# Layer 0's front reordered, and batch 1's second norm in smaller steps, in a two-layer transformer kernel on one core

## The chip, the core and the metric

The kernel runs on one core of a Trainium2 chip. The core has five engines that run side by side, each with its own in-order instruction queue: PE (TensorE, matrix products), DVE (VectorE, arithmetic on rows), ACT (ScalarE, functions and scaled copies), POOL (GpSimd, arithmetic on rows) and SP (SyncE, which here issues DMAs). PE writes to PSUM, a small memory of which the kernel uses eight banks; everything else lies in SBUF. DMA engines move data between the device's memory and SBUF, and also transpose tiles within SBUF. Loads and transposes are issued on SP's queue, weight loads on POOL's, and the stores of the result on ACT's.

The metric is the device time of the whole launch in microseconds (us), as the median of several runs; a profile is one execution more, with a record of every instruction.

## What is computed

Two batches of 1024 rows of 512 numbers pass through two layers. Each layer normalises its rows and adds an attention and a second branch to the input:

```python
xn = _layernorm(x)
x = x + _L0_attn_ref(xn, ...) + _L0_ffn_ref(xn, ...)
xn = _layernorm(x)
x = x + _L1_attn_ref(xn, ...) + _L1_ffn_ref(xn, ...)
```

Layer 0's attention has one head of width 128. Its second branch scales rows by their root mean square, forms 24 logits per row, runs 50 Sinkhorn steps on 16 of them (a 4 x 4 mixing matrix per row) and softmaxes on the others, and mixes four streams of 128 columns:

```python
x_norm = x * jax.lax.rsqrt(jnp.mean(x * x, axis=-1, keepdims=True) + RMS_EPS)
H_res = sinkhorn_log((x_norm @ W_res.T).reshape(B, T, n, n) + H_res_base)
y = jnp.einsum('btnc,btn->btc', x_streams, H_pre) @ W_branch
x_mixed = jnp.einsum('btij,btjc->btic', H_res, x_streams)
return (x_mixed + jnp.einsum('btc,btn->btnc', y, H_post)).reshape(B, T, nC)
```

Layer 1's attention has 32 query heads in 8 groups. Its queries attend over blocks of rows, causally; keys and values come from a compressed latent (`Wk_down`, `Wv_down`, then `Wk_up`, `Wv_up`). Its second branch is a dense product and a LoRA of 8 experts with two chosen per row by a small router (`gw1`, a norm, `gw2`, top 2); the router counts the rows of each expert over both batches and drops an expert's weights where a count is above the capacity:

```python
h = jax.nn.relu(layernorm(xf @ gw1.T + gb1) * ln_gamma + ln_beta)
top_v, top_i = jax.lax.top_k(h @ gw2.T + gb2, K)
counts = onehot.sum(axis=0)
allowed = (counts <= capacity).astype(xf.dtype)
main = xf @ weight.T
lora = jnp.einsum('enr,ero->no', tmp, lora_B) * ALPHA
```

## The kernel before

**Numbers.** Matrix operands are pairs of 16-bit halves, a high and a low part. A product is three passes (`mm3`, L89): high x high, high x low, low x high. So every operand costs a high part (a copy to 16 bits) and a low part (the difference). Weights are split on POOL by `split_pool` (L95 to L97: scale, high, low); results are split out of PSUM by `evac` (L105 on ACT, L106 on DVE).

**Tiles.** Each batch has eight tiles of 128 rows, kept in SBUF as `acc[b, t]`. A layer norm takes statistics of a tile (L220, L221), then parameters for several tiles at once (`layernorm_tiles`, L222 to L225, with `rsqrt`, L202 to L207: logarithm and exponential on ACT and one Newton step of four DVE operations). `normed_T` (L234 to L243) makes the normalised tile on ACT, POOL or DVE, its high part on ACT (L239), its low part on POOL or DVE (L241), and issues the transpose (L243) on SP's queue.

**Layer 0.** `front0` loads, normalises and transposes a batch (batch 0 in two halves of four tiles, `F0`), computes the 24 logits and the values V (L403, L106), then Q and K. `split_w0a` and `split_w0b` split the layer's weights; `lat_weights` loads (L674) and splits Wlat, which layer 1's latents use. `branch0` is the second branch's product with `W_branch` (PE, ACT L455, POOL L456 and L460), `branch0_add` adds it to the tiles on POOL (L469, L473). `attn0_rows` and `attn0_out` are the attention in two halves of 512 rows: scores, minimum of the negated scores (L288), exponential (L292), high part (L319 to L322), low part (L328 on POOL, L330 on DVE), transposes (L335), product with V, product with Wo, sum into `acc` (L506). The Sinkhorn iterations of batch 0 (`chain_dve`, L594 to L601) run on DVE, a step at a time between other work, with the matrix kept in a PSUM bank; those of batch 1 run on POOL during layer 1. After the chain, `mix0_units` mixes the streams of batch 0 (ACT L651, POOL L652, DVE L660), and the second norm of batch 0 follows in two halves (`LG`).

**Layer 1.** `layer1_attn` walks 16 groups (8 of each batch) of 32 steps; a step is `row_step`, 32 rows of four heads. Behind each step stands a list of other work at fixed places: projections, splits, the products with V and Wo, and everything in `extra`, entered by `put(h, s, f)` at step `s` counted from the start. So steps 192 to 223 are group 6, and 224 to 255 group 7, the last of batch 0. In this way batch 1's Sinkhorn chain and mixing, its second norm (`late_norm`, at step `LN1`), its router (tiles at `G1`, transposed tiles by `tile_of`, products `gating_h` three steps on by `GL`, ten steps of `gating`), the router's sum over both batches (`weights_of`, step `WT`), the transposed tiles that the attention needs (`xT_tile`, from `LX`), Wlat's splits (`lat_w`) and latents (`lat_unit`, from `LA`), and the dense branch's weights (`ffn_fetch`, `ffn_split`, `FW`) and blocks (`ffn_block`, `FF`) are all spread behind rows of batch 0.

**Order.** The program is written in this order, but a planner sorts the instructions of each engine before the launch; it may pull a ready instruction forward. Two tools bind it. `after(i)` lets what is written inside it be issued only behind `i`. `behind(i, j, True)` makes instruction `i` wait for `j`. `last_low` is the last low part made by DVE (L330). In `parts_of`, `mix0_units` and `ffn_split`, POOL's first operation already stands behind it.

**Buffers.** Tiles come from rings named by a tag: `f2k` has four buffers (weight staging, normalised tiles), `wo` nine, `xr` and `wq` four, `PT` three. In PSUM `pp` has three banks, `s` four, and `av` one, used by `out_tile`. A ring is handed out in the written order, so a new tile waits until the one that had its buffer before is read.

Of the kernel before, what the change touches and what calls it, by code (L numbers as in the profile page):

```python
# [16 lines left out]
P = 128  # L17
S = 1024
NB = 2
NT = S // P  # L20
# [19 lines left out]
SK0, SKN, MX0, MXN, LN1 = 1, 116, 122, 74, 198  # L40

G0, G1, GL, WT, LX, LA = 16, 200, 3, 220, 231, 240
# [3 lines left out]
FW, FF = 210, 221  # L46
# [6 lines left out]
def tile_model(ctx: ExitStack, tc: tile.TileContext, out: bass.AP, a: dict):  # L53
# [116 lines left out]
    def split_w0b():  # L170
        evac(st_qk, wqk0[:, :, 0, :], wqk0[:, :, 1, :], 8.0)
        A.activation(bqkv, bqkv, AF.Copy, scale=32.0)
        split_pool(st_o[:, 0:P], wb0[:, 0], wb0[:, 1], 32.0)
        split_pool(st_o[:, P:], wo0[:, 0], wo0[:, 1], 32.0)
        split_pool(bo_st, bo[:, 0], bo[:, 1], 32.0)
# [23 lines left out]
    def rsqrt(y, ve, tag):  # L199

        t = T(tag, list(ve.shape), bufs=2)
        A.activation(t, ve, AF.Ln)  # L202
        A.activation(y, t, AF.Exp, scale=-0.5)
        V.tensor_tensor(t, y, y, ALU.mult)
        V.tensor_tensor(t, t, ve, ALU.mult)
        V.tensor_scalar(t, t, -0.5, 1.5, ALU.mult, ALU.add)
        V.tensor_tensor(y, y, t, ALU.mult)  # L207
# [7 lines left out]
    def layernorm_tiles(b, mv, rs, ts):  # L215
        ve = T("ve", [P, NT], bufs=2)
        sl = slice(ts[0], ts[-1] + 1)
        for t in ts:
            st = T("bnst", [P, 6], bufs=2)
            V.bn_stats(st, acc[b, t])  # L220
            V.bn_aggr(mv[:, t, :], st)  # L221
        V.tensor_scalar(ve[:, sl], mv[:, sl, 1], LN_EPS, None, ALU.add)  # L222
        rsqrt(rs[:, 0, sl], ve[:, sl], "rs")
# [4 lines left out]
    def normed_T(b, mv, rs, t, dst, pool, tags=(("f2k", FB), ("wo", WB))):  # L228
# [6 lines left out]
        elif pool:  # L235
            G.tensor_scalar(xf, acc[b, t], rs[:, 2, t:t + 1], rs[:, 1, t:t + 1], ALU.mult, ALU.add)
# [4 lines left out]
        lo = eng.tensor_tensor(hl[:, :, 1, :], xn, hl[:, :, 0, :], ALU.subtract)  # L241
        (last_pool if eng is G else last_lo)[0] = lo
        last_T[0] = nc.sync.dma_start_transpose(dst, hl.rearrange("p c l d -> p (c l d)"))  # L243
# [126 lines left out]

    def front0(b, between=lambda: None):
        mv, rs = layernorm(b, "a")
        xT = T("xT", [P, NT, 2 * NC, P], F16, bufs=1)
        for ts in F0[b]:
            layernorm_tiles(b, mv, rs, ts)
# [13 lines left out]

        ms = T("rms", [P, NT], bufs=2)  # L390
        V.tensor_tensor(ms, rs[:, 0], rs[:, 0], ALU.mult)
        V.tensor_tensor(ms, ms, mv[:, :, 1], ALU.mult)
        V.tensor_scalar(ms, ms, RMS_EPS, None, ALU.add)
        rf = T("rf", [P, NT], bufs=2)
        rsqrt(rf, ms, "rs")
        V.tensor_scalar(rf, rf, 1.0 / 1024.0, None, ALU.mult)
        lg = T("lg", [P, NT, 24], bufs=1)
        Vh = T("V", [P, NT, 2, P], F16, bufs=2)
        for t in range(NT):
# [3 lines left out]
            V.scalar_tensor_tensor(lg[:, t, :], p[:, 128:152], rf[:, t:t + 1], base24,  # L403
                                   ALU.mult, ALU.add)
# [264 lines left out]
    def lat_weights():  # L669

        wl = T("PT", [P, 4, 2, NC, P], F16, bufs=3)
        for mc in range(4):
            st = T("f2k", [P, NC, P], bufs=FB)
            nc.gpsimd.dma_start(st, a["Wlat"][mc])  # L674
            split_pool(st, wl[:, mc, 0], wl[:, mc, 1], 32.0)
# [17 lines left out]
    def lat_w(mc):  # L693
        st = T("f2k", [P, NC, P], bufs=FB)
        nc.gpsimd.dma_start(st, a["Wlat"][mc])
        w1 = T("wo", [P, 2, NC, P], F16, bufs=WB)
        split_pool(st, w1[:, 0], w1[:, 1], 32.0)
        return w1
# [330 lines left out]
    def xT_tile(b, t, pool):  # L1029
        normed_T(b, *ln1[b], t, xT1[b][:, t], pool, (("f2k", FB), ("wo", WB)) if b else  # L1030
                 (("xr", XB), ("wo", WB)))

    def tile_of(b, t):
        d = T("wo", [P, 2 * NC, P], F16, bufs=WB)
        normed_T(b, *ln1[b], t, d, True, (("f2k", FB), ("xr", XB)))
# [28 lines left out]

    def late_norm():
        ln1[1] = layernorm(1, "b")
        layernorm_tiles(1, *ln1[1], range(NT))
# [14 lines left out]
    for t in range(NT):  # L1082
        for k, f in enumerate(mix0_units(1, t, f0[1][5], True)):
            put(0, MX0 + MXN * (4 * t + max(k - 1, 0)) // 32, f)
    for t in range(NT):
# [10 lines left out]
    for b, s in ((0, G0), (1, G1)):  # L1096
        put(0, s, lambda b=b: gate_start(b))
        for t in range(NT):
            if b == 0:
                put(0, s + t, lambda t=t: gating_h(hs[0], t, gw1, xT1[0][:, t]))  # L1100
            else:
                put(0, s + t, lambda t=t: dts.update({t: tile_of(1, t)}))
# [73 lines left out]
```

## Time and profile before

| | us |
|---|---|
| median of three runs (1847.12 to 1853.01) | 1851.1 |
| the profiled execution | 1847.95 |
| its span, first to last instruction | 1846.2 |
| PE busy | 1708.2 |
| DVE busy | 1473.1 |
| ACT busy | 1191.1 |
| POOL busy | 896.5 |

The mean granted clock of TensorE is 0.976 of full speed. Layer 0 takes about the first 223 us, and layer 1's rows the rest. Some marks on the way, each the start of an instruction group in the trace:

| | us |
|---|---|
| first statistics (L220) | 3.34 |
| first normalised tile (L238) | 15.04 |
| first transpose issued (L243) | 20.22 |
| first product of Q and K | 35.19 |
| first Sinkhorn operation of batch 0 (L527) | 38.50 |
| last Sinkhorn operation of batch 0 (L610) | 194.14 |
| PE starts layer 1's latents | 223.43 |
| parameters of batch 1's second norm ready (POOL starts L236) | 846.98 |
| first product of the dense branch | 921.88 |

A line of the page or the trace gives a start or a share, an engine, a line of the kernel, the operation, what it writes and reads with shapes, and in brackets how long the engine had been idle before and what ended that. In lines of stretches the columns are the stretch, its length, busy time and count of PE, PE's weight loads, DVE, ACT and POOL, then the granted clock, the DMA engines' share and GB/s. Where an operation line has a count above one, its duration is from the first start to the last end.

### The profile page before, as it was taken

Reading aid. Unit: us, or ns where it says so; the run is one execution under the profiler, and the core shown is the slowest. Engines: PE = TensorE matmul, PEld = TensorE weight load, DVE = VectorE, ACT = ScalarE, POOL = GpSimd, SP = SyncE. Lnnn points to the kernel's source line nnn. Section 1 sums busy time; section 2 is a strip of 40 time slices with the busy share of each in tenths; the row PEclk is TensorE's granted clock in tenths of the full one; section 3 lists DMA queues with packets and bytes.
Section 4 is the critical chain, followed back from the end, with each engine's and each line's share of the span. In section 5 each row is a group of like instructions: output and inputs, shape, how many; then the busy total and the mean of one; then the engine's idle time right before and its main releaser. Section 6 shows DMA issues by size and latency. Waiting matters only on the chain.

```text
span 1846.2 us, 35059 instructions
## 1 busy us (share of the span) xinstructions
PE 1708.2 (93%) x11394; PEld 1038.5 (56%) x11394; DVE 1473.1 (80%) x4162; ACT 1191.1 (65%) x2917; POOL 896.5 (49%) x1476
## 2 busy tenths in 40 slices
PE   4666389999999999998999999999999999999998
PEld 2434146566666566655555566666666666666565
DVE  8888968988888878778976768778787877787675
ACT  4848666656676778876544656667666767676564
POOL 5568629778766465647634433323242424235200
PEclk9888699999999999999999999999999999999999
DMA  7435225656575656468645656556566655566455
GB/s 212 82 56 132 59 44 123 151 118 139 119 149 98 141 128 144 105 142 143 146 98 125 144 126 140 135 124 141 125 134 124 142 118 142 124 143 135 97 121 118
DMA packets 693482, 230.25 MB, mean 125 GB/s; under 512 B 674081, under 2 KB 674209, under 8 KB 693298
## 3 DMA queue, kind: packets, MB, share of 16 engines
q1 hardware_dynamic: 677842, 180.75, 47.3%
q0 software_dynamic: 13152, 43.07, 8.7%
q10 hardware_dynamic: 2304, 4.20, 0.7%
q8 instruction: 89, 1.46, 0.3%
q14 instruction: 95, 0.78, 0.1%
HBM read 52.81 MB, written 4.19 MB: 31 GB/s over the span
## 4 chain that ended last, share of the span: by engine, by line
PE 47%; DVE 2%; DMA 1%; POOL 1%; issue 1%; ACT 0%; SPq 0%; DVEq 0%
PE pp L89 26%; PE av L365 11%; PE s L89 10%; DVE Phl L330 0%; DVE f2k L913 0%; DMA f2k<-in_Wq 0%; DMA xT<-wo 0%; DVE P L288 0%; POOL wo L241 0%; DMA PT<-Phl 0%; POOL f2k L95 0%; SPq L335 0%; DVE P L284 0%; DMA twT<-twhl 0%; DVE Q L106 0%
## 5 line engine op out<-in xcount | busy, mean ns | idle before, releaser
L292 ACT ACTIVATE P<-P,nm 128x1024 f32<-128x1024 f32 (+31 forms) x528 | 391.5, 742 | 280.9 <-DVE nm L284 263.4
L330 DVE SCALAR_TENSOR_TENSOR Phl<-P,r,Phl 128x64 f16<-128x64 f32 (+16 forms) x627 | 460.8, 759 | 75.7 <-ACT Phl L322 70.3
L89 PE MATMUL s<-K,Q 128*128 128x512 f16 (+22 forms) x2400 | 439.1, 317 | 19.7 <-DVE P L288 11.7
L365 PE MATMUL av<-PT,V 128*128 128x256 f16 x3456 | 425.6, 274 | 9.4 <-DMA PT<-Phl 8.5
L365 PEld LDWEIGHTS <-V 128*128 128x128 f16 x3456 | 338.2, 98 | 92.9 <-DMA PT<-Phl 10.6
L322 ACT ACTIVATE Phl<-P,r 128x1024 f16<-128x1024 f32 (+31 forms) x515 | 369.5, 730 | 20.6 <-DMA PT<-Phl 5.3
L89 PE MATMUL pp<-xT,wq 128*128 128x512 f16 x1536 | 371.8, 381 | 4.5 <-DVE Q L106 2.3
L89 PE MATMUL pp<-wo,ao 128*128 128x512 f16 x1536 | 369.9, 379 | 2.0 <-ACT ao L105 1.9
L95 POOL TENSOR_SCALAR f2k<-f2k 128x512 f32<-128x512 f32 x164 | 113.9, 695 | 500.6 <-DVE Phl L330 458.9
L89 PEld LDWEIGHTS <-Q 128*128 128x128 f16 x2400 | 222.8, 98 | 175.7 <-issue 27.7
L89 PEld LDWEIGHTS <-wq 128*128 128x128 f16 x1536 | 149.7, 98 | 172.6 <-issue 6.8
L89 PEld LDWEIGHTS <-ao 128*128 128x128 f16 x1536 | 149.5, 98 | 156.9 <-ACT ao L105 3.4
L284 DVE CUSTOM_DVE_ANT_0 P<-s,mask,nm 128x272 f32<-128x272 f32 (+15 forms) x256 | 157.3, 615 | 9.3 <-PE s L89 1.0
L288 DVE TENSOR_SCALAR_CACHE_REDUCE P<-s 128x512 f32<-128x512 f32 (+15 forms) x272 | 152.6, 562 | 13.4 <-PE s L89 11.2
L316 DVE RECIPROCAL r<-r 128x1 f32<-128x1 f32 x528 | 78.9, 154 | 87.5 <-ACT P L292 84.5
L317 ACT ACTIVATE r<-r 128x1 f32<-128x1 f32 x528 | 95.6, 192 | 60.2 <-DVE r L316 59.7
L105 ACT ACTIVATE ao<-av 128x512 f16<-128x512 f32 x128 | 74.9, 585 | 81.7 <-PE av L365 81.5
L334 POOL MEMSET Phl<- 128x192 f16 (+1 forms) x320 | 56.2, 189 | 142.3 <-DMA PT<-Phl 97.3
L105 ACT ACTIVATE Q<-pp 128x512 f16<-128x512 f32 x128 | 74.6, 583 | 64.3 <-PE pp L89 60.0
L284 DVE CUSTOM_DVE_ANT_0 P<-s,mask 128x32 f32<-128x32 f32 (+15 forms) x256 | 103.7, 430 | 14.9 <-PE s L89 14.2
L755 DVE SCALAR_TENSOR_TENSOR acc<-pp,acc 128x512 f32<-128x512 f32 x128 | 87.1, 681 | 35.1 <-PE pp L89 34.7
L106 DVE SCALAR_TENSOR_TENSOR Q<-pp,Q 128x512 f16<-128x512 f32 x128 | 87.4, 683 | 34.0 <-ACT Q L105 33.7
(256 smaller groups left out, 2153.1 us busy)
## 6 DMA issues: line engine op xcount, KB each, us to landing
f2k<-in_Wq POOLq DMA_DIRECT2D x64, 256.0 KB, 3.1
f2k<-in_WoT POOLq DMA_DIRECT2D x64, 256.0 KB, 3.3
PT<-Phl SPq DMA_TRANSPOSE x528, 3.2
acc<-in_x SPq DMA_DIRECT2D x16, 256.0 KB, 5.1
f2k<-in_Wup POOLq DMA_DIRECT2D x16, 256.0 KB, 3.3
out<-acc ACTq DMA_DIRECT2D x16, 256.0 KB, 3.5
xr<-V SPq DMA_DIRECT2D x32, 128.0 KB, 2.4
xr<-in_x SPq DMA_DIRECT2D x12, 256.0 KB, 3.9
```

Of the source, the lines that this page charges most:

```text
L89: nc.tensor.matmul(dst, lhs(l), rhs(r), start=(i == 0 and j == 0), stop=(i == n - 1 and j == 2))
L95: first = G.tensor_scalar(stage, stage, scale, 1.0, ALU.mult, ALU.mult)
L105: A.activation(hl_hi, src, AF.Copy, scale=scale)
L106: return V.scalar_tensor_tensor(hl_lo, src, scale, hl_hi, ALU.mult, ALU.subtract)
L284: last_row[0] = V.tensor_tensor_reduce(Pm[:, o:o + w], pt[:, :w], mask[:, 512 - w:], -scale, first, ALU.add, ALU.min, nm[:, k:k + 1])
L288: last_row[0] = V.tensor_scalar(Pm[:, o:o + w], pt[:, :w], -scale, first, ALU.mult, ALU.min, accum_out=nm[:, k:k + 1])
L292: A.activation(Pm[:, :W], Pm[:, :W], AF.Exp, bias=last, scale=-1.0, accum_out=r[:, 0:1])
L317: A.activation(r[:, 1:2], r[:, 1:2], AF.Copy, scale=PSCALE)
L322: A.activation(hl[1], Pm[:, :W], AF.Copy, scale=r[:, 1:2])
L330: last_low[0] = V.scalar_tensor_tensor(lo, Pm[:, a0:a1], r[:, 1:2], hi[:, a0:a1], ALU.mult, ALU.subtract)
L365: nc.tensor.matmul(p, v, pt, start=(k == 0), stop=(k == len(todo) - 1))
L755: V.scalar_tensor_tensor(acc[b, t], p, 1.0 / 256.0, acc[b, t], ALU.mult, ALU.add)
```

## The change

In layer 0's front:

- The loads of Wlat wait for the parameters of the first four tiles (`first_norm`), and the first operation of each of its splits waits for the last logits of batch 0 (`last_lg`). The splits of W_branch, Wo and bo wait for the same logits.
- The statistics of tiles 4 to 7 of batch 0 may be issued only behind the parameters of tiles 0 to 3.
- The root mean square's factor `rf` is computed right behind the last parameters, before the tiles that use them are normalised.
- `rsqrt` has a second form: the exponential goes to a tile in PSUM (tag `av`) and three `scalar_tensor_tensor` operations follow in place of four. `layernorm_tiles` uses it except for batch 1's second norm, and `rf` uses it.

In batch 1's second norm:

- The statistics of a tile are entered three steps after the last mixing step of the tile (`late_stats`); the parameters move from step 198 to 197.
- The router's tiles start at the steps of `G1` (198 to 207, one step left free at 202 and 206) and not at 200 to 207. Tiles 1, 4 and 7 are normalised on ACT (`GP`), the others on POOL, where they now stand behind `last_low`.
- `normed_T` has a second step, `later`: the low part and its transpose are entered one step further on; a low part on POOL stands behind `last_low`. This holds for the router's tiles and for `xT_tile` of batch 1.
- The ten steps of the router start at 210 and not at 211; `weights_of` moves from 220 to 221, the dense blocks from 221 to 222, the dense weights of batch 0 from 210 to 220 by twos to 210, 212, 213, 215, 216, 218, each fetched two steps earlier.
- Wlat's loads are entered two steps ahead of its splits, and the splits are made by `parts_of`, whose first operation stands behind `last_low`.

```diff
-SK0, SKN, MX0, MXN, LN1 = 1, 116, 122, 74, 198
-G0, G1, GL, WT, LX, LA = 16, 200, 3, 220, 231, 240
+SK0, SKN, MX0, MXN, LN1 = 1, 116, 122, 74, 197
+G0, GL, WT, LX, LA = 16, 2, 221, 231, 240
+G1 = (198, 199, 200, 201, 203, 204, 205, 207)
+GP = (1, 2, 1, 1, 2, 1, 1, 2)
+G2 = 210
-FW, FF = 210, 221
+FW, FF = ((210, 212, 213, 215, 216, 218), tuple(8 * 58 + 2 + 2 * k for k in range(6))), 222
...
-        split_pool(st_o[:, 0:P], wb0[:, 0], wb0[:, 1], 32.0)
-        split_pool(st_o[:, P:], wo0[:, 0], wo0[:, 1], 32.0)
-        split_pool(bo_st, bo[:, 0], bo[:, 1], 32.0)
+        for args in ((st_o[:, 0:P], wb0[:, 0], wb0[:, 1]), (st_o[:, P:], wo0[:, 0], wo0[:, 1]),
+                     (bo_st, bo[:, 0], bo[:, 1])):
+            behind(split_pool(*args, 32.0), last_lg[0], True)
...
-    def rsqrt(y, ve, tag):
+    def rsqrt(y, ve, tag, ps=False):
...
+        if ps:
+            r = out_tile()[:, :ve.shape[1]]
+            A.activation(t, ve, AF.Ln)
+            A.activation(r, t, AF.Exp, scale=-0.5)
+            V.scalar_tensor_tensor(t, r, -0.5, ve, ALU.mult, ALU.mult)
+            V.scalar_tensor_tensor(t, r, 1.0, t, ALU.mult, ALU.mult)
+            V.scalar_tensor_tensor(y, t, 1.5, r, ALU.add, ALU.mult)
+            return
...
+    def layernorm_tile(b, mv, t):
+        st = T("bnst", [P, 6], bufs=2)
+        V.bn_stats(st, acc[b, t])
+        V.bn_aggr(mv[:, t, :], st)
+
+    def layernorm_tiles(b, mv, rs, ts, late=False):
...
+        for t in () if late else ts:
+            layernorm_tile(b, mv, t)
         V.tensor_scalar(ve[:, sl], mv[:, sl, 1], LN_EPS, None, ALU.add)
-        rsqrt(rs[:, 0, sl], ve[:, sl], "rs")
+        rsqrt(rs[:, 0, sl], ve[:, sl], "rs", not late)
...
-            G.tensor_scalar(xf, acc[b, t], rs[:, 2, t:t + 1], rs[:, 1, t:t + 1], ALU.mult, ALU.add)
+            xg = G.tensor_scalar(xf, acc[b, t], rs[:, 2, t:t + 1], rs[:, 1, t:t + 1], ALU.mult, ALU.add)
+            if later is not None:
+                behind(xg, last_low[0], True)
...
+        def low():
+            lo = eng.tensor_tensor(hl[:, :, 1, :], xn, hl[:, :, 0, :], ALU.subtract)
+            if eng is G and later is not None:
+                behind(lo, last_low[0], True)
+            (last_pool if eng is G else last_lo)[0] = lo
+            last_T[0] = nc.sync.dma_start_transpose(dst, hl.rearrange("p c l d -> p (c l d)"))
+
+        if later is None:
+            low()
+        else:
+            later(low)
...
         for ts in F0[b]:
-            layernorm_tiles(b, mv, rs, ts)
+            with after(*stt):
+                stt = [layernorm_tiles(b, mv, rs, ts)]
+            first_norm.append(stt[0])
+            if ts[-1] == NT - 1:
...
+                rsqrt(rf, ms, "rs", True)
...
-            nc.gpsimd.dma_start(st, a["Wlat"][mc])
-            split_pool(st, wl[:, mc, 0], wl[:, mc, 1], 32.0)
+            load = nc.gpsimd.dma_start(st, a["Wlat"][mc])
+            first = split_pool(st, wl[:, mc, 0], wl[:, mc, 1], 32.0)
+            behind(load, first_norm[0], True)
+            behind(first, last_lg[0], True)
...
+        put(0, MX0 + MXN * (4 * t + 3) // 32 + 3, lambda t=t: late_stats(t))
...
-                put(0, s + t, lambda t=t: dts.update({t: tile_of(1, t)}))
-                put(0, s + t + GL, lambda t=t: gating_h(hs[1], t, gw1, dts[t]))
+                put(0, G1[t], lambda t=t: dts.update({t: tile_of(1, t, lambda f: lows.update({t: f}))}))
+                put(0, G1[t] + 1, lambda t=t: lows.pop(t)())
+                put(0, G1[t] + GL + 1, lambda t=t: gating_h(hs[1], t, gw1, dts[t]))
...
-        put(0, LX + t, lambda t=t: xT_tile(1, t, t % 2 == 1))
+        put(0, LX + t, lambda t=t: xT_tile(1, t, t % 2 == 1, lambda f: lows.update({t: f})))
+        put(0, LX + t + 1, lambda t=t: lows.pop(t)())
...
-        put(0, LA + 2 * mc - 4, lambda mc=mc: lw.update({mc: lat_w(mc)}))
+        put(0, LA + 2 * mc - 6, lambda mc=mc: lw.update({mc: fetch(a["Wlat"][mc])}))
+        put(0, LA + 2 * mc - 4, lambda mc=mc: lw.update({mc: lat_w(lw[mc])}))
```

## The prediction

> **What bounds the kernel now.** I read the page's 40 slices first, then the busy time by stretches, then what PE (TensorE) waits for, then the instructions of single stretches in order of time.
>
> ```profile
> PE   4666389999999999998999999999999999999998
> DVE  8888968988888878778976768778787877787675
> sum 360.00, PE 248.88 PEld 145.19 DVE 308.33 ACT 220.27 POOL 231.27; mean PE 10.82 PEld 6.31 DVE 13.41 ACT 9.58 POOL 10.06
> 200.00:220.00 20.00, 0.00 (x0) 0.00 (x0) 19.16 (x60) 17.29 (x55) 14.13 (x12) 0.50 0.19 37
> ...
> sum 290.00, PE 275.12 PEld 162.92 DVE 224.76 ACT 172.33 POOL 147.29; mean PE 9.49 PEld 5.62 DVE 7.75 ACT 5.94 POOL 5.08
> ```
>
> PE is busy 1708.2 of 1846.2 us, so 138 us idle can be had at all. The first sum covers 0 to 360 us: PE idle 360 - 248.9 = 111 us there, with DVE (VectorE) at 308 of 360 and at 19.16 of 20 where PE stands still altogether. The second covers 790 to 1080: 14.9 us idle. From 1050 on PE is full, so nothing after that can gain. Layer 0 (the first 223 us) is bound by DVE, whose 50-step Sinkhorn chain of batch 0 fills every gap from 38.5 to 194.1 us; the second limit there, ending at nearly the same time (L506's last sum from 193.59), is the attention path through ACT, POOL and SP. The change touches the start of the first stretch and 820 to 1050 of the second.
>
> ```profile
> 13.04 1.15 POOL L97 TENSOR_TENSOR PT<-f2k,PT 128x512 f16<-128x512 f32 x1
> 13.08 1.13 DVE L207 TENSOR_TENSOR rsa<-rsa,rs 128x4 f32<-128x4 f32 x1
> 15.04 2.02 DVE L238 TENSOR_SCALAR wq<-acc,rsa 128x512 f32<-128x512 f32 x2
> 20.22 11.79 SPq L243 DMA_TRANSPOSE xT<-wo  x8
> 35.19 10.52 PE L89 MATMUL pp<-xT,cmp 128*128 128x512 f16 x48
> 132.64 1.16 POOL L439 TENSOR_TENSOR Q<-f2k,Q 128x512 f16<-128x512 f32 x1 [10.07 <-ACT Q L438]
> 132.64 0.29 DVE L599 TENSOR_TENSOR sk<-s,sk 128x128 f32<-128x128 f32 x1
> ```
>
> A four-element multiply takes 1.13 us when POOL runs a tensor op from the same moment; undisturbed it is 0.15 to 0.17 (211.41: 0.16). L599, whose first operand is in PSUM, keeps its 0.29 beside a POOL op. So DVE stalls in the front are POOL's weight splits. The first normalised tile starts at 15.04, the first transpose is issued at 20.22, Q and K start at 35.19.
>
> ```profile
> 850.04 3.41 DVE L330 SCALAR_TENSOR_TENSOR Phl<-P,r,Phl 128x352 f16<-128x352 f32 x1
> 850.79 2.27 POOL L241 TENSOR_TENSOR xr<-f2k,xr 128x512 f16<-128x512 f32 x2
> 861.22 4.44 PE L89 MATMUL pp<-xT,wq 128*128 128x512 f16 x12 [2.22 <-DVE acc L755]
> 921.88 2.81 PE L89 MATMUL pp<-cmp,xT 128*128 128x128 f16 x13 [0.84 <-POOL cmp L96]
> 934.49 0.17 PE L946 MATMUL pp<-ch,ones 128*128 128x16 f16 x1 [1.07 <-DVE ch L940]
> 935.37 0.83 PE L89 MATMUL pp<-cmp,xT 128*128 128x128 f16 x12 [0.71 <-DVE al L948]
> ```
>
> Late: a low part L330 of 352 columns takes 3.41 us (its 384-column neighbours were three in 3.19) while POOL makes low parts of normalised tiles; then PE waits 2.22 us and runs 12 matmuls in 4.44 us where 2.75 is usual at full clock (832.35).
>
> **Part A, the front.** Removed from 9 to 17 us: POOL's Wlat splits and the early 1 MB of Wlat loads, which shared the DMA with x (273 GB/s in the first 10 us; 256 KB take 0.96 us of that). The statistics of tiles 4 to 7 go behind the first four's parameters, and rsqrt has three DVE ops, reading PSUM, for four. New sum: fourth x tile at about 6.2, its statistics 0.69 + 0.17 to 7.05, L222 0.15, Ln and Exp with their hand-overs 0.65, three ops at 0.2, L224 and L225 0.35: parameters at about 9.0 instead of 15.0. DVE then has 1.1 (two L238 at 0.55), 3.4 (four statistics), 0.85 (split_w0a), 1.4 to 2.4 (two L241): second parameters at some 17.3 instead of 22.6. The last low part is POOL's; from 28.5 it comes to about 22.5. So the transposes, Q and K move by 5.5 us (35.2 to 29.7), and the last logits, which now find rf ready, by 7.5 (37.8 to 30.3).
>
> Given back: POOL's splits now start behind the last logits: Wlat 4 x (0.62 + 0.62 + 1.15) = 9.6, Wbo and bo 6.7 by their rows from 28.48 to 35.01. Some 16 us, 30 to 46, over an engine that was idle from 35.0 to 49.4. There DVE has ten small SBUF ops (L180, L222, L419, L423, L425, L527, L531, L535, L537, L541), each exposed to half a POOL op (0.4): +4, between 0 and 10 x 1.15 = 11.5. Queued behind the splits on POOL are branch0's adds L456 (from 49.39; by then it is through, so nothing). The Wlat loads wait on POOL's queue for the parameters; POOL has nothing else then, and Wlat's matmuls come at 223 us: nothing, and if that cover went a load costs 5.7 us. The rsqrt result lives in the single av bank; batch 1's allocation comes after the second attention output of batch 0, whose bank is read at 97.46, so its parameters can't come at 48 to 53 any more but at some 93 to 100, beside POOL's adds (98.9 to 122.6). Batch 1's first tile is normalised at 108.96 behind POOL, which hides it; five small ops there lose half of 1.15: +2, between 0 and 6. The chain on DVE thus gains 7.5 - 4 - 2 = 1.5, the attention path 5.5. Since DVE sets the end I take **-2**, with -7.5 and +4 as ends.
>
> The Trainium skill ("SBUF — State Buffer", section "Who interferes with whom") says that a DVE op with two SBUF inputs contends with a GpSimd op that reads SBUF and is blocked for that whole op, one with at most one SBUF input outside the two-port modes is not. The rows 13.08 and 132.64 agree, and it speaks against this change: moved splits meet the two-input ops of Sinkhorn's start. By its whole-op wording alone the give-back would be 11.5 and the front a loss.
>
> **Part B, parameters of the second norm, batch 0.** L204 to L225 took 209.37 to 211.97 and 227.00 to 229.79. Three PSUM ops at 0.2 and two at 0.17 are 1.0: -1.6 in the first, which PE waits for (its idle ends at 223.43 after 30 us). In the second PE has work until 233, then waits 3.54: I count -0.4. **-2**, ends -3.2 and 0.
>
> **Part C, late.** Statistics tile by tile: seven of eight are already taken between 646 and 804 as POOL's adds finish, with 2.2 us of DVE idle in three waits: nothing, at worst those 2.2. Tiles: three of eight move their first op (0.76 to 1.8 on POOL) to ACT (L234, 0.8); ACT is busy 7.4 of 10 there: nothing. What is moved on queues: six FFN and four Wlat fetches go one to two steps ahead on POOL's queue (0.56 to 0.59 of issue each, 3.3 to 5.7 to land), eight transposes one step back on SP's (1.25 each); the longer-held buffers are of f2k's four. Gating reads a tile two steps after its transpose, which hides them: nothing, and if the buffers run out, part of rival 3. POOL's parts now wait for a low part of DVE, so that they don't run into L330. Candidates: the wait at 861 (2.22 and 4.44 - 2.75 of slow clock: 3.9), FFN splits up to two steps earlier (0.84), the router's sum and the FFN one step later (1.07 + 0.71), transposes and Wlat fetched earlier at 1009 to 1017 (0.77 + 1.21): 8.5. DVE is busy 39.8 of 40 us between 900 and 940 with the gating work unchanged, so I take half: **-4**, ends -8.5 and (below) +10.
>
> The Trainium skill ("TensorE: Matmul & The Clock Gate", section "Why this matters for your kernels") asks only for gaps under about 3 us. Here a gap of 2.22 us was followed by matmuls at a low clock, so the trace differs; by the page the 861 term would be 2.2, and the part -3.
>
> **Sum.** The three parts give -2 - 2 - 4 = -8 against the profiled execution's 1847.95 (span 1846.2 and 1.75 around it): 1840. The median of the three runs is 1851.1, 3.15 above that execution, so the median forecast is **1843**, its own range 1838 to 1846.
>
> **Rivals.** (1) The front is swallowed: DVE's total work from 38 to 194 decides, contention only moves from 9-30 to 30-46, and the late region is bound by DVE's gating at 900 to 940. Only part B and about 1 us stay: 1848. For it: DVE 95 to 98% busy at 50 us and at 900 to 940. Against: the front holds over 8 us of inflated ops.
> (2) The attention path sets layer 0's end, and POOL kept off L330 gives all: -5.5 - 2 - 8 = 1835.5. For it: POOL is never idle 98.9 to 122.6 on that path. Against: the chain's last product starts at 194.14, behind the last output's sum.
> (3) Slower: the new waits block POOL's queue. Five first parts and eight low parts now wait; queued behind them on POOL are the splits and fetches of Wq, Wo, Wup and the FFN, for which PE waits in order. POOL's adds L652 that already have such waits idled 50.2 us over 14, 3.6 each. POOL is busy 30.3 of 40 us at 840 to 880, so 9.7 can be absorbed and about 6 more from FFN splits brought forward. At 2 us each 26 are wanted: +10, with -4 of the rest 1857; it decides from (9.7 + 6) / 13 = 1.2 us per wait. Against: each waits for the low part of the step just before it, which by data is earlier than the tile.
> That the change does nothing is unlikely only for the front; for the statistics it holds.
>
> **How the numbers follow.** Forecast 0.45, rival 1 0.20, rival 2 0.13, rival 3 0.22. What can be told from no change is 0.3%, 5.5 us: below 1845.6 is faster (0.45 + 0.13 = 0.58), rival 1 the same (0.20), rival 3 slower (0.22). All terms at their good ends give -19.2, 1832; I stop at 1833, and at rival 3's 1857: eight in ten.
>
> **What would show it.** Right: L238 first at 9 to 10, Q and K at 29 to 31, no rsqrt op over 0.6 us before 30, L403 done by 31, PE's first long run (223.43) at 218 to 221, no L330 over 2 us between 840 and 880, no twelve matmuls above 3 us at 861. Wrong: DVE ops of 0.6 to 1.2 between 30 and 46 that add up to more than 6; the long run not earlier than 222; POOL waiting on L330 for more than 16 us at 840 to 880 and PE on POOL's splits after it.

## The result, and the profile after

The changed kernel takes 1855.52 us (median of 15 runs, 1851.67 to 1861.01); the kernel before, run beside it, 1850.62. The ratio is 1.0029, with a 95% interval of 1.0019 to 1.0039. A second measurement beside other kernels gave 1853.64 against 1850.78, 1.0016 (1.0004 to 1.0027). So it is slower by 0.2 to 0.3%, some 4 us, where 1843 was forecast. The profiled execution took 1860.26 us (span 1858.4), 4.7 above its median; that of before lay 2.7 below its own. The two profiles differ by 12.3 us, of which only some 3 to 5 are the change's; a second profile of the same changed kernel took 1853.27.

First the stretches, PE, PE's weight loads, DVE, ACT and POOL, then clock, DMA share and GB/s. Before:

```profile
850.00:900.00 50.00, 47.78 (x390) 29.24 (x387) 40.68 (x101) 29.37 (x69) 36.14 (x52) 0.97 0.77 164
...
1000.00:1080.00 80.00, 78.02 (x483) 44.79 (x481) 60.38 (x143) 50.45 (x107) 39.91 (x62) 1.00 0.71 165
```

and after:

```profile
850.00:900.00 50.00, 43.52 (x363) 27.20 (x361) 35.82 (x94) 27.46 (x64) 29.77 (x43) 0.97 0.74 138
...
1000.00:1080.00 80.00, 71.45 (x413) 40.10 (x412) 60.69 (x137) 47.39 (x106) 37.01 (x57) 0.96 0.74 148
```

PE was busy 4.3 us less at 850 to 900 and 6.6 less at 1000 to 1080. Next the front of the changed kernel, as instructions in order of time:

```profile
10.32 0.99 DVE L255 TENSOR_SCALAR wq<-acc,rsa 128x512 f32<-128x512 f32 x2
...
15.86 11.00 SPq L264 DMA_TRANSPOSE xT<-wo  x8
...
30.00 10.52 PE L92 MATMUL pp<-xT,cmp 128*128 128x512 f16 x48
...
30.98 0.88 POOL L98 TENSOR_SCALAR P<-P 128x128 f32<-128x128 f32 x2 [7.46 <-DVE lg L435]
...
38.22 0.92 DVE L455 TENSOR_TENSOR hh<-hh,hmx 128x64 f32<-128x64 f32 x1
...
41.32 4.58 POOL L100 TENSOR_TENSOR PT<-f2k,PT 128x512 f16<-128x512 f32 x4
```

The tiles, the transposes, and Q and K come some 5 us earlier than before (30.00 for 35.19); rsqrt's three operations on PSUM take 0.16 us each. POOL starts its splits the moment the last logits are there and runs through to 46 us, and DVE's small SBUF operations beside it take up to 0.92 us (L455, 0.19 before). Now PE's waits and what followed them, late; first three of before, then the changed kernel's:

```profile
930.95 2.47 PE L365 MATMUL av<-PT,V 128*128 128x256 f16 x21 [1.44 <-DMA PT<-Phl]
...
1009.82 0.59 PE L89 MATMUL pp<-xT,wo 128*128 128x512 f16 x2 [0.77 <-issue]
...
1017.12 2.75 PE L89 MATMUL pp<-xT,wo 128*128 128x512 f16 x12 [1.21 <-DMA xT<-wo]
```

```profile
858.25 0.47 PE L92 MATMUL pp<-gw,wo 128*128 128x32 f16 x12 [1.71 <-DVE acc L785]
...
860.16 2.75 PE L92 MATMUL pp<-xT,wq 128*128 128x512 f16 x12
...
879.83 0.50 PE L92 MATMUL pp<-gw,wo 128*128 128x32 f16 x12 [3.21 <-DMA wo<-xr]
...
935.51 4.66 PE L391 MATMUL av<-PT,V 128*128 128x256 f16 x21 [4.25 <-DMA PT<-Phl]
...
1017.19 1.47 PE L391 MATMUL av<-PT,V 128*128 128x256 f16 x12 [2.29 <-DVE ao L109]
...
1025.27 2.74 PE L391 MATMUL av<-PT,V 128*128 128x256 f16 x12 [6.20 <-DMA PT<-Phl]
```

The twelve slow matmuls of 861 are fast: 2.75 us at 860.16. The wait in front of them is not gone: PE waits 1.71 us at 858.25 for the same one of DVE's sums (L785; L755 in before, where it was 2.22), now in front of a product of the router. In addition PE waits for the router's transposed tiles (`wo<-xr`; 4.8 us in three waits), 4.25 us for the attention's at 935 (before 1.44 at 931), and 8.5 us at 1017 and 1025, where before lost 2.0.

### The profile page after: what moved, and what is told of

Its sections match the earlier page's. It is cut to its first block, busy times and chain, and to the rows that moved or that the text cites. A ratio compares the mean times of both kernels' runs of the same rounds, so it can differ in the third digit from the quotient of the medians.

```text
span 1858.4 us, 35051 instructions
## 1 busy us (share of the span) xinstructions
PE 1713.8 (92%) x11394; PEld 1041.3 (56%) x11394; DVE 1469.6 (79%) x4155; ACT 1193.4 (64%) x2920; POOL 890.5 (48%) x1473
## 5 line engine op out<-in xcount | busy, mean ns | idle before, releaser
L318 ACT ACTIVATE P<-P,nm 128x1024 f32<-128x1024 f32 (+31 forms) x528 | 391.6, 742 | 298.1 <-DVE nm L310 279.1
L356 DVE SCALAR_TENSOR_TENSOR Phl<-P,r,Phl 128x64 f16<-128x64 f32 (+16 forms) x627 | 461.2, 760 | 74.7 <-ACT Phl L348 68.2
L360 POOL MEMSET Phl<- 128x192 f16 (+1 forms) x320 | 55.8, 187 | 158.7 <-DMA PT<-Phl 95.9
L785 DVE SCALAR_TENSOR_TENSOR acc<-pp,acc 128x512 f32<-128x512 f32 x128 | 87.2, 681 | 34.2 <-PE pp L92 33.8
L100 POOL TENSOR_TENSOR wo<-f2k,wo 128x512 f16<-128x512 f32 x84 | 102.5, 1222 | 4.3
```

Of the source, the lines that this page charges most:

```text
L100: G.tensor_tensor(hl_lo, stage, hl_hi, ALU.subtract)
L318: A.activation(Pm[:, :W], Pm[:, :W], AF.Exp, bias=last, scale=-1.0, accum_out=r[:, 0:1])
L356: last_low[0] = V.scalar_tensor_tensor(lo, Pm[:, a0:a1], r[:, 1:2], hi[:, a0:a1], ALU.mult, ALU.subtract)
L785: V.scalar_tensor_tensor(acc[b, t], p, 1.0 / 256.0, acc[b, t], ALU.mult, ALU.add)
```

## The experiments

All ratios are against the kernel before, run on the same chip at the same time, with 95% intervals. Two marks help to place a loss, since single executions of one program differ by several us: the start of PE's first long run in layer 1 (223.43 in before; mark A), and the time from the 47th to the 65th of DVE's 128 sums of layer 1 (L785, in before L755), which are at 842.31 and 1117.58 in before (275.3; mark B). A line number of an experiment's kernel can differ by a few from that of the changed kernel.

**The change in halves.** e1 keeps the front and the PSUM form of rsqrt, and everything late is as before; e2 is the reverse.

```diff
-SK0, SKN, MX0, MXN, LN1 = 1, 116, 122, 74, 197
+SK0, SKN, MX0, MXN, LN1 = 1, 116, 122, 74, 198
...
-G1 = (198, 199, 200, 201, 203, 204, 205, 207)
-GP = (1, 2, 1, 1, 2, 1, 1, 2)
+G1 = tuple(range(200, 208))
+GP = (True,) * 8
...
```

> The change's front and its PSUM form of rsqrt (also in the second norm of batch 0), with everything late as before. Theory (the front holds its gain of about 2 us up to layer 1, the late part loses): 2 to 3 us below the kernel before, some 1848, and PE's long run starts at 223 to 225. Rival (the front itself loses, by POOL's moved splits and the low clock behind the waits at 70 and 179 us, and the late part is worth nothing): 3 to 6 us above before, near the changed kernel's 1855.5.

> The change's late part alone, with front and rsqrt as before. Theory: 6 to 8 us above before (1857 to 1859), with the waits for transposes at 875 to 880, 917 to 936 and 1017 to 1031 seen again. Rival (the front loses): within 2 us of before. Rival (the two parts meet, and the late part suffers from a shifted schedule of the front): within 2 us, too, but then the front alone is also near before.

Measured: e1 0.9985 (0.9970 to 1.0000), e2 1.0019 (1.0005 to 1.0033). The front gains a little, some 2.8 us (its interval reaches to nothing), and the late part alone loses some 3.5. So the wrong sign comes from the late part. In e1 the wait at 861 is as in before:

```profile
861.46 4.03 PE L92 MATMUL pp<-xT,wq 128*128 128x512 f16 x12 [3.20 <-DVE acc L789]
```

**One step for two.** In e3 the low part and transpose follow at once, for the router's tiles (shown) and for xT's.

```diff
-                put(0, G1[t], lambda t=t: dts.update({t: tile_of(1, t, lambda f: lows.update({t: f}))}))
-                put(0, G1[t] + 1, lambda t=t: lows.pop(t)())
+                put(0, G1[t], lambda t=t: dts.update({t: tile_of(1, t, lambda f: f())}))
...
```

> The changed kernel, but the low part and the transpose of a router tile and of a tile of xT are entered in the same step as the normalisation; waits on POOL, steps and all else stay. Theory (transposes entered a step late stand at the head of SP's queue while they wait for their low parts, and hold the attention's transposes): 4 to 7 us below the changed kernel, 1849 to 1851.5, and PE's waits for transposes at 870 to 880 and 1017 to 1031 are gone. Rival (POOL's new waits are the cause): within 1.5 us of the changed kernel. Rival (the two steps do help): up to 5 us slower than it.

Measured: 1.0018 (1.0001 to 1.0035), and the wait at 1016 is 6.87 us. My first theory, that the transposes entered a step late block SP, fell: with one step the loss stays.

**Without POOL's new waits.** e4 drops both `behind` in `normed_T`.

```diff
-                behind(xg, last_low[0], True)
...
-                behind(lo, last_low[0], True)
```

> The changed kernel without the waits of POOL's normalisations and low parts for DVE's last low part; the two steps stay. Theory (SP's queue): within 1.5 us of the changed kernel, 1854 to 1857, a little slower where POOL meets L356 again at 850. Rival (the waits block POOL's queue): 5 to 8 us below it, 1848 to 1850, and POOL's idle stretch of 12 us at 875 to 887 is gone.

Measured: 0.9990 (0.9975 to 1.0005). Without these waits the changed kernel is no slower than before, which is near the third rival of the prediction; the later runs show that they aren't the whole of the loss. But POOL's idle stretch, which I had named as the sign, only fell from 12 to 6.9 us, so that stretch wasn't the way.

**Which of them.** e5 is the changed kernel again. e6 (shown) keeps the waits for the tiles of xT alone, e7 those for the router's tiles alone, e8 only those of the normalisations.

```diff
-            if later is not None:
+            if later is not None and tags[1][0] == "wo":
                 behind(xg, last_low[0], True)
...
-            if eng is G and later is not None:
+            if eng is G and later is not None and tags[1][0] == "wo":
                 behind(lo, last_low[0], True)
```

> The changed kernel unaltered, beside the next three runs on one chip: 0.2 to 0.4% above before. It shows which of its waits come back in a second profile: the one of 6.2 us on PE for the attention's transposes at about 1025 should (theory: it comes from POOL's waits for the tiles of xT); the one of 3.2 at 880 may not (rival: chance in the transfers).

> The changed kernel without the new waits on the router's tiles, but with those on the tiles of xT. Theory X (the waits on xT's tiles cost: at 1000 to 1030 POOL's pads and low parts come late, SP's transposes stand behind them): as slow as the changed kernel, within 2 us of it, with a PE wait of 4 to 7 us at about 1020. Theory R (the waits on the router's tiles cost, at 850 to 880): 4 to 6 us below the changed kernel, near the 1849.9 of the run without any of them.

> The changed kernel without the new waits on the tiles of xT, but with those on the router's tiles. Theory X: 4 to 6 us below the changed kernel, near 1849.9, and PE waits no longer than some 4 us at about 1020. Theory R: within 2 us of the changed kernel.

> The changed kernel with the waits on POOL's normalisations kept and those on its low parts taken away, for router and xT alike. If the low parts' waits cost (they stand ahead of the pads and splits in POOL's queue): 4 to 6 us below the changed kernel. If the late normalisations cost (a tile that starts late ends late): within 2 us of it.

Measured: e5 1.0016 (1.0004 to 1.0027), e6 1.0020 (1.0004 to 1.0037), e7 1.0006 (0.9994 to 1.0018), e8 1.0008 (0.9995 to 1.0020). The intervals overlap; the medians point to the waits for xT's tiles and, by e8, to those of the low parts, but don't show it. PE's long waits there, first e6, then e7:

```profile
1021.05 2.74 PE L391 MATMUL av<-PT,V 128*128 128x256 f16 x12 [6.15 <-DMA PT<-Phl]
```

```profile
1015.37 1.87 PE L391 MATMUL av<-PT,V 128*128 128x256 f16 x12 [3.69 <-DMA PT<-Phl]
```

The changed kernel itself had 6.20 in one profile and, in e5, 1.97 in the other: this wait comes and goes between executions. The first one's DVE and POOL, and then SP, show how it came about:

```profile
1015.75 0.79 DVE L356 SCALAR_TENSOR_TENSOR Phl<-P,r,Phl 128x544 f16<-128x544 f32 x1 [0.50 <-ACT Phl L348]
```

```profile
1016.88 0.61 POOL L99 TENSOR_SCALAR wo<-f2k 128x512 f16<-128x512 f32 x1 [3.15 <-issue]
1017.47 0.61 POOL L98 TENSOR_SCALAR f2k<-f2k 128x512 f32<-128x512 f32 x1
1018.05 1.14 POOL L260 TENSOR_TENSOR wo<-f2k,wo 128x512 f16<-128x512 f32 x1
1019.16 1.14 POOL L100 TENSOR_TENSOR wo<-f2k,wo 128x512 f16<-128x512 f32 x1
1020.25 0.25 POOL L360 MEMSET Phl<- 128x192 f16 x1
```

```profile
1002.85 13.53 SPq L264 DMA_TRANSPOSE xT<-wo  x6
1016.43 4.81 SPq L361 DMA_TRANSPOSE PT<-Phl  x2
1021.34 1.96 SPq L264 DMA_TRANSPOSE xT<-wo  x1
```

The attention's low part is ready at 1016.54, but the zeros that fill its last 192 columns (L360) come at 1020.25: they stand on POOL's queue behind operations of two splits and the low part of the last tile of xT (L260). The transpose waits for them on SP, whose row ends at 1021.24. Without the wait for DVE's low part (e4), the planner puts the same zeros ahead of that low part: they are at 1006.94 there, the low part at 1008.01, and PE waits 4.09 us in place of 6.20.

**The pads on DVE.** A pad is the part of a row that is filled with zeros before it is transposed. e12 keeps all waits and clears the pads on DVE for 14 steps.

```diff
-            behind(G.memset(pad, 0.0), last_low[0])
+            if pads_on_dve[0]:
+                V.memset(pad, 0.0)
+            else:
+                behind(G.memset(pad, 0.0), last_low[0])
...
+    put(0, LX, lambda: pads_on_dve.__setitem__(0, True))
+    put(0, LX + 14, lambda: pads_on_dve.__setitem__(0, False))
```

> The changed kernel, all waits kept, but in the 14 steps from the first tile of xT the pads of the attention's low parts are cleared on DVE and not on POOL. Theory (POOL's waits cost because the pads stand behind the waiting low parts and splits in POOL's queue, and the attention's transposes wait for the pads): the PE wait at about 1020 falls from 2 to 7 us to below 3 in the profile, and the time is 2 to 4 us below the changed kernel. Rival (the late xT transposes themselves hold SP): the wait stays, and the time is within 1.5 us of the changed kernel.

Measured: 0.9990 (0.9973 to 1.0008), 0.26 and 0.39% below the changed kernel's two ratios, and the PE wait at 1015.72 is 3.06 us. That is at least the gain that was expected, with one doubt: the planner also put one of the attention's transposes ahead of the last one of xT, as in e4, so pad and order are not separated.

**More time for the router's transposes.** e9 reads a tile three steps after its transpose is entered; e10 drops xT's waits too.

```diff
-G0, GL, WT, LX, LA = 16, 2, 221, 231, 240
+G0, GL, WT, LX, LA = 16, 3, 221, 231, 240
-G2 = 210
+G2 = 211
```

> The changed kernel with the router's products three steps after a tile's transpose is entered, not two (GL 3, and the router's ten steps from 211). Theory (two steps are too few: PE waits 3 to 5 us in all for the router's tiles at 857 to 880, which takes the place of the wait at 861): those waits fall below 1.5 us, and the time is 2 to 4 us below the changed kernel (0.0 to 0.1% above before). Rival (850 to 940 is bound by DVE, so what PE waits for there is indifferent): the waits go, PE waits as long for others, and the time stays within 1.5 us of the changed kernel.

> The same, and POOL's waits for the tiles of xT taken away as well. Theory: both losses gone, 4 to 7 us below the changed kernel, at 0.1 to 0.2% below before, as the front alone. Rival: no better than the run with the router's waits only (0.06% above before).

Measured: e9 0.9987 (0.9971 to 1.0002), e10 0.9999 (0.9984 to 1.0014). e9 gained more than the theory had it; the reason is not borne out: PE's waits for the router's tiles are still 4.4 us in all, in four (read in the slowest of its twelve executions, 1856.45 us). And with xT's waits gone as well nothing more is won. What made e9 faster than the changed kernel stays open, and it speaks against the waits for xT's tiles as a sure cost: e9 has them all.

**The moved splits.** e11 is e1 with the splits of W_branch, Wo and bo free to run early.

```diff
-            behind(split_pool(*args, 32.0), last_lg[0], True)
+            split_pool(*args, 32.0)
```

> The change's front alone, but POOL's splits of W_branch, Wo and bo don't wait for the last logits. If the splits that were moved to 30 to 46 us give back some 4 us by contention with DVE, as predicted: fewer DVE operations above 0.4 us between 31 and 46, the first scores 1 to 3 us earlier than 46, and 1 to 2 us below the front alone (1848 to 1849). If the contention costs nothing at layer 0's end, because the attention path sets it: within 1 us of the front alone (0.15% below before).

Measured: 0.9965 (0.9951 to 0.9980), 1847.55 us: faster than before and than the change. POOL's and then DVE's rows:

```profile
28.75 1.14 POOL L100 TENSOR_TENSOR wo<-Q,wo 1x512 f16<-1x512 f32 x1
31.47 2.47 POOL L98 TENSOR_SCALAR f2k<-f2k 128x512 f32<-128x512 f32 x4 [1.58 <-DVE lg L435]
...
36.28 4.55 POOL L100 TENSOR_TENSOR PT<-f2k,PT 128x512 f16<-128x512 f32 x4
```

```profile
44.66 0.68 DVE L314 TENSOR_SCALAR_CACHE_REDUCE P<-s 128x512 f32<-128x512 f32 x1
```

The three splits end at 29.9, Wlat's at 40.8 and not at 45.9, and the first scores are read at 44.66 (46.09 in the changed kernel). Eight small operations on SBUF at the start of DVE's Sinkhorn and softmax work take 1.9 us in all in before, where POOL was idle beside them, 5.3 in the changed kernel and 3.7 in e11. Mark A says it more strongly: 224.5 on average in eleven profiles with the moved splits (221.9 to 228.7), 220.7 in six with early ones (219.6 to 221.5), 223.4 and 225.1 in the two with the old front. So of 3.8 us at mark A, DVE's operations account for 1.6; what makes up the rest was not traced.

**What is left of the late part.** f1 has both repairs (early splits, no waits for xT). f2 and f3 are e11 with one part of the late change each: the dense branch's weights, the sum and the blocks; or the statistics and the router's tiles. g1 and g2 halve f2; their edits are shown against e11.

```diff
# g1
-FW, FF = (tuple(210 + 2 * k for k in range(6)), tuple(8 * 58 + 2 + 2 * k for k in range(6))), 221
+FW, FF = ((210, 212, 213, 215, 216, 218), tuple(8 * 58 + 2 + 2 * k for k in range(6))), 221
# g2
-G0, GL, WT, LX, LA = 16, 2, 220, 231, 240
+G0, GL, WT, LX, LA = 16, 2, 221, 231, 240
...
-FW, FF = (tuple(210 + 2 * k for k in range(6)), tuple(8 * 58 + 2 + 2 * k for k in range(6))), 221
+FW, FF = (tuple(210 + 2 * k for k in range(6)), tuple(8 * 58 + 2 + 2 * k for k in range(6))), 222
```

> The changed kernel with W_branch's, Wo's and bo's splits free of the wait for the last logits, and without POOL's new waits for the tiles of xT. Theory (the front without the moved splits is worth 0.35%, and the late part without the waits for xT's tiles loses some 0.14%): 0.15 to 0.3% below before, 1847 to 1850, not faster than the front alone with the early splits. Rival (the late part without those waits gains its 4 us): 0.5% below before.

> The front with early splits, and of the late part the dense branch's weights, blocks and the router's sum at their new steps alone. Theory (no wait that PE loses at 900 to 940 is worth time, for DVE is full there; POOL's splits, brought into that stretch, lengthen DVE's low parts): the waits at 918 to 937 change place, and the time is the front's, 0.25 to 0.4% below before, or up to 2 us above it. Rival (as predicted): 1 to 2 us below the front alone, 0.4 to 0.5% below before.

> The front with early splits, and of the late part the statistics, the router's tiles in two steps with their waits, and the router's ten steps alone. Theory (the wait for the sum at 861 gives way to waits for the router's transposes): no wait of 2 to 3 us at 857 to 862 followed by slow matmuls, 3 to 5 us of waits for the router's tiles in its place, and a time 1 to 3 us above the front alone (0.2 to 0.3% below before). Rival (as predicted): 2 to 4 us below the front alone.

> The front with early splits, and of the late part only the earlier steps of the dense weights' loads and splits (210, 212, 213, 215, 216, 218). The planner's order differs from the front's in 188 lines on PE and in 2 on SP. Theory O (the loss of the dense part is one of order: the sum and the blocks one step later rearrange PE, DVE and SP from 900 to 1060): within 2 us of the front alone (0.35% below before). Theory W (the loads meet the router's transposes on the DMA engines at 860 to 880 and POOL's splits meet DVE's low parts): 3 to 9 us above the front alone.

> The front with early splits, and of the late part only the router's sum at step 221 and the dense blocks from 222, each one step later; the weights as before. The planner's order differs from the front's in 1272 lines on PE and in 15 on SP. Theory O: 5 to 9 us above the front alone (0.0 to 0.15% above before), with PE's wait for the attention's transposes at 930 at 3 to 4 us and more of PE idle at 1000 to 1060. Theory W: within 2 us of the front alone. As predicted (1.07 and 0.71 us of waits gone): 1 to 2 us below it.

| kernel | ratio | 95% interval | mark B, us |
|---|---|---|---|
| e11, late as before | 0.9965 | 0.9951 to 0.9980 | 276.7 |
| g1, dense weights earlier | 0.9997 | 0.9982 to 1.0012 | 278.3 |
| g2, sum and blocks later | 0.9993 | 0.9977 to 1.0010 | 279.1 |
| f2, both | 1.0016 | 1.0004 to 1.0028 | 282.1 |
| f3, router's tiles | 0.9978 | 0.9966 to 0.9989 | 279.6 |
| f1, all without xT's waits | 0.9997 | 0.9986 to 1.0009 | 279.2 |

Against e11 each half of the dense part costs some 0.3%, about 5 us, both 0.5%, the router's tiles 0.1%, by ratios whose own intervals are 0.11 to 0.17% to either side; the 0.1% is not clear of them. Neither theory, O or W, was right alone, and the forecast of a gain failed in both halves. The parts don't add up to the whole (f1 is better than f2); why is open. One place where g1 and e11 differ, DVE, POOL and PE of g1, in this order:

```profile
924.79 2.10 DVE L356 SCALAR_TENSOR_TENSOR Phl<-P,r,Phl 128x928 f16<-128x928 f32 x1
```

```profile
924.75 1.15 POOL L100 TENSOR_TENSOR wo<-f2k,wo 128x512 f16<-128x512 f32 x1
```

```profile
927.52 4.66 PE L391 MATMUL av<-PT,V 128*128 128x256 f16 x21 [3.13 <-DMA PT<-Phl]
```

and DVE and PE of e11 at the same place:

```profile
923.67 1.18 DVE L356 SCALAR_TENSOR_TENSOR Phl<-P,r,Phl 128x928 f16<-128x928 f32 x1
```

```profile
928.97 2.47 PE L391 MATMUL av<-PT,V 128*128 128x256 f16 x21 [1.75 <-DMA PT<-Phl]
```

A low part of one of Wo's splits on POOL, which now finds the dense weights' splits out of its way, meets a DVE low part, which takes 2.10 us and not 1.18; PE waits 1.4 longer for it, and the 21 matmuls then run at the low clock, 2.2 longer. This doesn't show where g1's 5 us go. In e11 the same POOL operation comes at 928.30 and meets DVE's next low part (960 columns), which takes 2.12 there and 1.57 in g1; and the profiled execution of g1, the fastest of its twelve, took 1846.72 us against 1847.32 of e11's. The planner's order differs in both halves too (188 lines on PE in g1, 1272 in g2) and isn't separated from the moves. How the dense part's two halves cost time stays open.

**Batch 1's parameters.** f4 is e11 with rsqrt in SBUF for batch 1's first norm and its `rf`.

```diff
-                stt = [layernorm_tiles(b, mv, rs, ts)]
+                stt = [layernorm_tiles(b, mv, rs, ts, ps=b == 0)]
...
-                rsqrt(rf, ms, "rs", True)
+                rsqrt(rf, ms, "rs", b == 0)
```

> The front with early splits, and batch 1's first norm with rsqrt in SBUF as before, so that its parameters don't wait for the one bank of the attention's products. If they cost 2 us at 93 to 100, as predicted: these operations go back to about 50, and the time is 1 to 2 us below the front with early splits. If DVE has the time, because the attention path sets layer 0's end: within 1 us of it.

Measured: 0.9966 (0.9954 to 0.9978), 1844.82 us against 1850.87, as e11's ratio. Mark A is at 219.2, 2.3 earlier than e11's. Whether these parameters cost something can't be told from the times; e11 and f4 are the fastest versions found, 0.35% below before.

## Why the prediction was wrong

**The step that failed is the sum of part C**, "so I take half: **-4**". The late part alone cost 3.5 us (e2), and about 7 by difference: 0.23% above before for the whole change (mean of the two measurements) less -0.15% for e1 is 0.38%. Part C's ends had +10 as the upper one, and so the whole range held 1855.5, but the sign of the likeliest case was wrong. One by one:

- The wait at 861 (3.9): the 1.7 us of slow clock went, but of the wait's 2.22 us 1.71 stayed, at 858. "Gating reads a tile two steps after its transpose, which hides them: nothing" failed: in the profiles with the new router's steps PE waits 2.5 to 5.3 us in all for these tiles, with the old ones 0 to 2.8 (0 in before, 1.0 in e1). In f3, which has them alone, the waits are 1.77, 0.45 and 3.04. One wait was traded for others.
- "FFN splits up to two steps earlier (0.84)": the 0.84 went as foreseen (0.41 is left in the changed kernel), but g1, which has this edit alone, is some 0.3%, about 5 us, slower than e11. I had seen that DVE is full at 900 to 940 and drew from it only that half be taken. By what way the earlier splits cost time is open.
- "The router's sum and the FFN one step later (1.07 + 0.71)": g2 loses as much. In its profile the wait for DVE's `ch` (1.07 in before) is gone, the one for `al` is 1.70 at 936 in place of 0.71, and PE lost time at 930 (a wait of 2.53 us followed by 21 matmuls in 4.13) and in four waits at 1008 to 1023 (3.9 in all, 1.8 in e11).
- "Transposes and Wlat fetched earlier (0.77 + 1.21)": these 2.0 us became 3.6 to 8.7 in the profiles where the waits for xT stand, and 2.9 to 5.0 in those of the late part without them; with the late part as before they are 1.8 to 2.8.
- "Eight transposes one step back on SP's queue": priced at nothing, and e3 bears it out.

**Rival 3 was near the cause of one of the losses, by the wrong route.** I counted 13 new waits, five first parts and eight low parts: those are the router's tiles' alone. The eight on xT's tiles (four first parts and four low parts on POOL) were left out, and they are the ones to which e6 and e7 point. I priced the waits by what is queued behind them and counted splits and fetches, at 840 to 880. Where one is seen to cost, it is at 1000 to 1030, and by a thing that I had left off the list: the pads of the attention, quarter-microsecond operations on which SP's transposes wait. By mark B, six profiles with the late part and xT's waits took 280.6 on average (275.1 to 285.5), six in which those waits or their effect were taken away 276.8 (273.9 to 279.6), and four with the late part as before 276.2 (275.3 to 277.4). So these waits seem to be worth some 4 us, with groups that overlap and with e9's time against it. The rest of the late part gains nothing by this mark, and by time it loses 0.3% (f1 against e11), most clearly in the dense branch's new steps.

**The front.** Its mechanism held in nearly all its signs: first parameters from 9.04, Q and K at 30.0, no rsqrt operation above 0.2 us, logits done at 30.9; the normalised tile, at 10.32, missed 9 to 10 by a little. "+4" given back to the moved splits is near what DVE's eight operations show, 3.4 us (5.3 for 1.9). Moving those of W_branch, Wo and bo back is worth 3.8 us by mark A and 0.2% in time (e1 against e11), though Wlat's splits still overlap DVE in e11 and DVE gets back only 1.6. With the give-back the front as written is worth 0 by mark A and 2.8 us, from 0 to 5.5, by e1's time; parts A and B together were put at -4. The +2 for the av bank is not settled. The long run "at 218 to 221" failed for the change (224.87); in the six profiles with early splits it is at 219.6 to 221.5.

**Signs.** No L356 (L330 in before) took over 2 us at 840 to 880 and no twelve matmuls were slow there, as said; both were true and no sign of a gain, for they named the place of the old wait only. The eight lengthened DVE operations at 30 to 46 make 5.3 us, below the 6 that I had set, and the long run was later than 222, a sign of being wrong that came true. POOL did not wait 16 us at 840 to 880.

**The cited rules.** The Trainium skill, "SBUF — State Buffer" ("Who interferes with whom"), spoke against the moved splits. The changed kernel's rows agree with it: beside POOL's splits L455, with two SBUF inputs, takes 0.92 us for 0.19, while L474, which reads one input from PSUM, keeps its 0.74; and e11 is faster. The Trainium skill, "TensorE: Matmul & The Clock Gate" ("Why this matters for your kernels"), asks for gaps below about 3 us. Here 2.2 to 2.5 us were enough several times (2.17 and 2.22 in before, 2.53 in g2), though 2.19 in e9 was not, and in the changed kernel 1.82 at 179 us, soon after a gap of 3.96. The measurement decides.

## What to carry to other kernels

Where an engine that feeds PE is full, don't price a wait of PE by its length: here moving work by a step or two, to remove a wait of 0.84 us in one place and of 1.07 and 0.71 in another, came with a loss of about 5 us each. Before making an instruction wait, list everything behind it on its in-order queue, down to the smallest operation, and ask whose DMA needs that. Before moving weight splits on POOL, look at what DVE does at the new place: beside them its small operations on two SBUF inputs took up to five times as long here, those that read PSUM did not. And compare profiles only with their own executions' times beside them: g1's profile is its fastest execution, e9's its slowest.

## What the runs showed of the hardware

- The low clock turns small waits into larger ones. A group of 21 of the attention's matmuls takes 2.45 to 2.47 us at full clock. After a wait of 1.75 us (e11) it took 2.47, after 2.19 (e9) 2.47, after 2.53 us (g2) 4.13, after a dozen waits between 3.1 and 4.5 us 3.8 to 4.7. The profiles' records of the granted clock hold only full and half speed, and the stretches at half, but for the last one at a trace's end, are 3.4, 6.8, 10.2 us and so on: multiples of 3.41. So a wait costs whole steps or none; that it depends on where the wait falls on this grid would explain why 2.17 us cost one and 2.19 none, but wasn't tested.
- At the end of layer 0 this took back what was left of the front's gain. POOL's last low part comes 1.5 us earlier than before (174.12 for 175.63), but the 24 matmuls that follow ran at half clock, and the next sum is 0.7 us later (before, then after):

```profile
180.38 2.78 PE L365 MATMUL av<-PT,V 128*128 128x256 f16 x24 [1.51 <-DMA PT<-Phl]
```

```profile
179.18 4.69 PE L391 MATMUL av<-PT,V 128*128 128x256 f16 x24 [1.82 <-DMA PT<-Phl]
```

  From that low part to the next sum of the output it is 7.8 us in both profiles with the old front and 9.1 to 10.9 in all eighteen with the new one. Why the clock should be worse there each time wasn't settled.
- One program's executions differ by 6 to 15 us from the fastest to the slowest, and one profile may hold a wait of 6 us that the next doesn't have. A loss is placed by several profiles, not by one.
